# Attention of 32 heads in row blocks of 4 heads x 32 queries instead of 1 head x 128 queries, with the output projection per 128 tokens of all four heads

## The chip, the core and the metric

The kernel runs on one core of one Trainium2 chip, in one launch. The metric is the time of an execution on the device in microseconds (us). The time of the kernel before is 1990.96 us, the median of three runs (1986.2 to 1993.41). The engines are called PE (TensorE, matrix products), DVE (VectorE), ACT (ScalarE), POOL (GpSimd) and SP (SyncE, which here only issues DMAs). Lines such as L83 are lines of the kernel before.

## The reference

The model has two layers over x of 2 batches x 1024 tokens x 512. Layer 0 adds to the normed input's residual a single-head attention (d = 128) and a mixture of four streams, whose weights come from 50 Sinkhorn iterations. Layer 1 adds a grouped causal attention and a feed-forward block with eight low-rank experts, of which each token takes two. Nearly all of the time goes into the attention of layer 1: 32 query heads of 128, in 8 groups of four heads that share keys and values.

```python
def _L1_attn_ref(hidden_states, Wq, Wk_down, Wv_down, Wk_up, Wv_up, Wo):   # 2 x 1024 x 512
    H, HK, D = (32, 8, 128)
    q = (hidden_states @ Wq.T).reshape(b, s, H, D).transpose(0, 2, 1, 3)
    ...                       # k, v: down to 256 latent values, up to 8 heads of 128
    k = jnp.repeat(k, n_rep, axis=1)          # n_rep = 4
    v = jnp.repeat(v, n_rep, axis=1)
    scores = jnp.einsum('bhqd,bhkd->bhqk', q, k) * scale
    scores = jnp.where(causal, scores, jnp.asarray(-1000000000.0, scores.dtype))
    attn = jax.nn.softmax(scores, axis=-1)
    out = jnp.einsum('bhqk,bhkd->bhqd', attn, v)
    out = out.transpose(0, 2, 1, 3).reshape(b, s, H * D)
    return out @ Wo.T
xn = _layernorm(x, axis=-1)
x = x + _L0_attn_ref(xn, ...) + _L0_ffn_ref(xn, ...)
xn = _layernorm(x, axis=-1)
x = x + _L1_attn_ref(xn, ...) + _L1_ffn_ref(xn, ...)
```

## The kernel before

**Products.** Every product is made of three float16 passes over operands that are split into a high and a low part: high x high, high x low, low x high (`mm3`, L78 to L85). A result is taken out of PSUM by an eviction (`evac`, L97 to L99): ACT writes the high part, DVE the low part. Weights arrive as float32, by DMAs that POOL issues, and POOL splits them with three instructions (`split_pool`, L87 to L91: scale, high, low).

**A row step of attention** (`row_step`, L297 to L309) works on 128 partitions, which are 128 queries of one head. Block i of a head has 128(i+1) keys, so eight steps have widths 128, 256, ..., 1024.

1. `rows_scores` (L238): PE writes the scores into one or two PSUM tiles of up to 512 columns; there are four such tiles (tag `s`).
2. `rows_exp` (L251): DVE negates the scores and takes the running minimum, with the causal mask at the last piece (L260) and without it at an earlier one (L264). ACT takes the exponential and its sum (L268).
3. `rows_hi` (L272): DVE takes the reciprocal of the sum (L273), ACT scales it (L274) and writes the high part of the normed row, `Phl` (L281).
4. `rows_lo` (L284): DVE writes the low part (L290). A transposing DMA on SP (L292) brings the blocks of 128 x 128 of both parts to `PT`, with keys on the partitions.

A step issues its own scores and exponential together with the normalising (3 and 4) of the step before: first 1, then 3 for the older one, then 2, then 4 for the older one.

**Attention times V** (`attn_out`, L311) has V as weights and 512 queries of a head's half as moving columns: 12 products for the first half (keys up to 512) and 24 for the second, where the causal limit cuts the width to 512, 384, 256 or 128. `PTa` and `PTb` hold the transposed rows of the two halves, one buffer each. `head_av` (L631) evicts the result to `AO`.

**Layer 1** (`layer1_attn`, L637 to L711) goes through 64 heads (two batches), eight steps a head. Everything else is hung to a step ("slot") of a head by `at`, and `put` in the program does the same for work of other stages: the weight and the projection of the next head's Q (`load_q`, `q_half`), attention times V after slots 6 and 14 of a head, the next group's keys and values (`kv_next`) in the third head of a group, and, after the fourth head, eight blocks of the output projection (`wo_block`, L622: 12 products of 512 columns over the four heads' `AO`, then an addition to `acc` on DVE, L627, and in the last group the output's DMA on ACT's queue, L629). A batch thus has 8 groups of 32 row steps; G0 to G7 are batch 0, G8 to G15 batch 1.

**The program** (L822 to L903) runs layer 0's front for both batches, the Sinkhorn iterations of batch 0 on DVE, the stream mix, and the latents; those of batch 1's Sinkhorn (on POOL), its stream mix, its normalisation and the expert blocks are hung into the slots of layer 1. Between the batches (G7 to G8) the normed activations of batch 1 (`xT`) are made, and their latents.

**Order.** The tile framework orders the instructions of each engine when the kernel is built, by a timeline of its own (L947), from the order in which the code issues them, their dependencies and the free buffers. On the chip each engine works through its list in that order.

Of the kernel before, what the change touches and what calls it, by code (L numbers as in the profile page):

```python
# [9 lines left out]
F16 = mybir.dt.float16  # L10
# [6 lines left out]
P = 128  # L17
S = 1024
NB = 2
# [9 lines left out]
FB, HB, PB, LB, XB = 4, 4, 3, 3, 4  # L29
# [9 lines left out]
QA, QB, QNA, QNB, AA, AB = 0, 4, 4, 4, 6, 14  # L39
WA, WB, KV, KVN, LQ, LW = 12, 16, 4, 13, 5, 5  # L40
# [6 lines left out]
def tile_model(ctx: ExitStack, tc: tile.TileContext, out: bass.AP, a: dict):  # L47
    """Products run as three float16 passes over operands split into a high and
    a low part (hi*hi + hi*lo + lo*hi), each scaled by a power of two."""
# [25 lines left out]
    # passes over (lhs part, rhs part)  # L75
    PASSES = ((0, 0), (0, 1), (1, 0))

    def mm3(dst, pairs):  # L78
        """dst += sum over pairs of lhsT.T @ rhs, in three passes each."""
# [7 lines left out]
    def split_pool(stage, hl_hi, hl_lo, scale):  # L87
        """stage is scaled in place; its parts go to hl_hi and hl_lo."""
        G.tensor_scalar(stage, stage, scale, 1.0, ALU.mult, ALU.mult)  # L89
        G.tensor_scalar(hl_hi, stage, 1.0, 1.0, ALU.mult, ALU.mult)  # L90
        G.tensor_tensor(hl_lo, stage, hl_hi, ALU.subtract)  # L91
# [11 lines left out]
    # ---------------------------------------------------------- constants  # L103
    mask = C("mask", [P, 512])
    G.memset(mask, 0.0)
    G.affine_select(mask[:, 384:512], mask[:, 384:512], [[-1, P]],
# [3 lines left out]
    pm = C("pm", [P, 8])           # 8 - e  # L110
# [10 lines left out]
    # first layer's operands  # L121
# [13 lines left out]
    wo0 = T("wo", [P, 2, H], F16, bufs=4)  # L135
# [16 lines left out]
    bo = T("wo", [1, 2, H], F16, bufs=4)  # L152
# [8 lines left out]
    def split_w0b():  # L161
# [5 lines left out]
        # g = 1/(1+exp(-gate)), 1-g = exp(-gate) g; both over 4, for 4*xn  # L167
# [5 lines left out]
    # ---------------------------------------------------------- helpers  # L173
# [3 lines left out]
    def after(*insts):  # L177
        """issues what follows behind each of insts on its engine."""
# [5 lines left out]
    def rsqrt(y, ve, tag):  # L184
        """y = ve ** -0.5; ve > 0."""
# [8 lines left out]
    def layernorm(b, tag):  # L194
        """rows of acc[b, :]: mean and variance, 1/std, -4 mean/std, 4/std."""
# [17 lines left out]
    def normed_T(b, mv, rs, t, dst, pool, tags=(("f2k", FB), ("h2k", HB))):  # L213
        """dst[p, 2c+part, tok] of 4*(x-mean)/std."""
# [15 lines left out]
    def proj_T(w, xT, half):  # L230
        """psum[m, tok] of one half of the tokens; w(c, part) is [128 f, m]."""
# [6 lines left out]
    def rows_scores(Q, K, i, causal):  # L238
        """scores of the query rows of block i: (offset, width, psum) pieces."""
        W = P * (i + 1) if causal else S  # L240
        pieces = [(0, W)] if W <= 512 else [(0, W // 2), (W // 2, W // 2)]
        got = []
        for o, w in pieces:
            count[0] += 1
            pt = ps.tile([P, 512], F32, tag="s", name=f"s_{count[0]}", bufs=BS)
            mm3(pt[:, :w], [(lambda l: Q[:, l, i * P:(i + 1) * P],
                             lambda r: K[:, r, o:o + w])])
# [3 lines left out]
    def rows_exp(pieces, causal, scale):  # L251
        """exp(score - max) and its sums."""
# [19 lines left out]
    def rows_hi(Pm, r, W, pool):  # L272
        V.reciprocal(r[:, 1:2], r[:, 0:1])  # L273
        A.activation(r[:, 1:2], r[:, 1:2], AF.Copy, scale=PSCALE)  # L274
        hl = T("Phl", [P, NT, 2, P], F16, bufs=LB)
        p3 = Pm[:, :W].rearrange("p (j k) -> p j k", k=P)
        if pool:
            A.activation(Pm[:, :W], Pm[:, :W], AF.Copy, scale=r[:, 1:2])
            A.activation(hl[:, :W // P, 0, :], p3, AF.Copy)
        else:  # L280
            A.activation(hl[:, :W // P, 0, :], p3, AF.Copy, scale=r[:, 1:2])  # L281
        return hl

    def rows_lo(Pm, r, W, pool, hl, dst):  # L284
        n = W // P
        p3 = Pm[:, :W].rearrange("p (j k) -> p j k", k=P)
        if pool:
            G.tensor_tensor(hl[:, :n, 1, :], p3, hl[:, :n, 0, :], ALU.subtract)
        else:
            V.scalar_tensor_tensor(hl[:, :n, 1, :], p3, r[:, 1:2], hl[:, :n, 0, :],  # L290
                                   ALU.mult, ALU.subtract)
        nc.sync.dma_start_transpose(dst[:, 0:2 * n, :],  # L292
                                    hl[:, :n].rearrange("p j l k -> p (j l k)"))
# [3 lines left out]
    def row_step(Q, K, i, causal, scale, dst, pool):  # L297
        """one block of rows, a step ahead of the normalising of the last one."""
        if Q is not None:
            pieces = rows_scores(Q, K, i, causal)  # L300
        if pending:
            *what, d = pending.pop()
# [648 lines left out]
```

## Time and profile before

| what | value |
|---|---|
| median of three runs | 1990.96 us (1986.2, 1990.96, 1993.41) |
| the profiled execution's own time | 1993.41 us |
| its span | 1993.4 us |
| G0's first score product | 297.7 us after the span's start |
| G1 to G7, first score products | 391.7, 490.8, 587.2, 688.9, 799.7, 890.1, 1001.9 us |
| G8 (batch 1) to G15 | 1168.0, 1261.4, 1358.6, 1454.7, 1550.7, 1648.1, 1745.0, 1841.0 us |
| last product of PE | ends at 1989.6 us |

The profile is one execution. Its busy times by engine say how full an engine is; the slices say when. A group of instructions has the line, the engine, the operation, what it writes and reads with partitions x elements, a count, its busy time and the mean of one, and then the idle time of that engine just before those instructions, with what ended most of it. Some groups join several widths ("+3 forms"). The chain of work that ended last begins with these shares:

```profile
PE 33%; DVE 28%; issue 12%; ACT 12%; DMA 10%; POOL 5%; SPq 0%; DVEq 0%; ACTq 0%; POOLq 0%
```

Two rows of DMA issues matter for the change. Their columns are the transfer, the queue, the operation, the count and the median time from issue to landing in us:

```profile
PTb<-Phl SPq DMA_TRANSPOSE x272, 3.6
...
PTa<-Phl SPq DMA_TRANSPOSE x256, 2.6
```

### The profile page before, as it was taken

What the parts mean: (1) busy time and instruction counts of PE and PEld (TensorE: products, weight loads), DVE (VectorE), ACT (ScalarE), POOL (GpSimd) and SP (SyncE); (2) the same over time, 40 slices, a digit from 0 to 9 for tenths busy, and PEclk for the clock granted to TensorE, in tenths of its full rate; (3) what the DMA queues carried; (4) which work ended last, traced back from release to release, by engine and by line L of the source; (5) the groups of instructions that cost most, each with busy time, mean ns of one, the idle gap of its engine ahead of it and who ended that gap; (6) DMA issues with size and microseconds to landing.
All of it is one profiled execution on the core that took longest, in us unless ns stands there. A gap on an engine that the chain in (4) does not pass through costs nothing.

```text
span 1993.4 us, 32134 instructions
## 1 busy us (share of the span) xinstructions
PE 1779.4 (89%) x10210; PEld 920.4 (46%) x10210; DVE 1570.5 (79%) x4340; ACT 1219.5 (61%) x2902; POOL 871.7 (44%) x1178
## 2 busy tenths in 40 slices
PE   4365389899999998999999799999999999999998
PEld 2223134445455444554545355454545454545454
DVE  8999969988888787778875757777777777777755
ACT  3445456567576888674663646766666666666543
POOL 6644585866666656234710634141514142326010
PEclk9777699999999998999999999999999999999999
DMA  7131354656555565566643836555556575656524
GB/s 197 32 73 28 79 113 88 144 116 133 126 121 122 116 132 111 106 133 132 145 104 65 182 95 149 116 123 120 121 119 138 105 135 110 138 117 151 102 55 125
DMA packets 707293, 230.08 MB, mean 115 GB/s; under 512 B 689953, under 2 KB 690081, under 8 KB 707122
## 3 DMA queue, kind: packets, MB, share of 16 engines
q1 hardware_dynamic: 691666, 180.75, 44.1%
q0 software_dynamic: 13152, 43.07, 8.3%
q10 hardware_dynamic: 2304, 4.20, 0.6%
q8 instruction: 81, 1.33, 0.3%
q14 instruction: 90, 0.74, 0.1%
HBM read 52.81 MB, written 4.19 MB: 29 GB/s over the span
## 4 chain that ended last, share of the span: by engine, by line
PE 33%; DVE 28%; issue 12%; ACT 12%; DMA 10%; POOL 5%; SPq 0%; DVEq 0%; ACTq 0%; POOLq 0%
PE pp L83 19%; PE av L319 8%; PE s L83 6%; DVE Phl L290 6%; DMA PTb<-Phl 5%; ACT Phl L281 5%; DVE P L260 4%; ACT P L268 4%; DVE P L264 4%; DVE sk L501 2%; DVE sk L507 2%; DMA PTa<-Phl 2%; DVE acc L544 1%; DVE sk L512 1%; DVE sk L493 1%
## 5 line engine op out<-in xcount | busy, mean ns | idle before, releaser
L268 ACT ACTIVATE P<-P,nm 128x1024 f32<-128x1024 f32 (+7 forms) x528 | 412.3, 781 | 374.8 <-DVE nm L260 338.7
L290 DVE SCALAR_TENSOR_TENSOR Phl<-P,r,Phl 128x1024 f16<-128x1024 f32 (+7 forms) x520 | 492.3, 959 | 161.9 <-ACT Phl L281 160.2
L83 PE MATMUL s<-K,Q 128*128 128x384 f16 (+5 forms) x2400 | 486.9, 333 | 71.3 <-DVE P L264 49.1
L281 ACT ACTIVATE Phl<-P,r 128x1024 f16<-128x1024 f32 (+7 forms) x520 | 399.3, 777 | 65.9 <-DMA PTb<-Phl 44.4
L83 PE MATMUL pp<-xT,wq 128*128 128x512 f16 x1632 | 381.4, 380 | 4.7 <-POOL wq L91 2.2
L83 PE MATMUL pp<-wo,AO 128*128 128x512 f16 x1536 | 361.2, 380 | 1.4 <-DVE acc L627 0.7
L83 PEld LDWEIGHTS <-Q 128*128 128x128 f16 x2400 | 227.4, 99 | 276.1 <-issue 98.8
L319 PE MATMUL av<-PTb,V 128*128 128x512 f16 (+3 forms) x1632 | 325.0, 348 | 13.7 <-DMA PTb<-Phl 11.2
L319 PEld LDWEIGHTS <-V 128*128 128x128 f16 x2400 | 229.0, 99 | 234.4 <-issue 26.0
L83 PEld LDWEIGHTS <-wq 128*128 128x128 f16 x1632 | 158.0, 98 | 175.5 <-POOL wq L91 3.0
L83 PEld LDWEIGHTS <-AO 128*128 128x128 f16 x1536 | 149.7, 98 | 167.2 <-issue 3.9
L89 POOL TENSOR_SCALAR f2k<-f2k 128x512 f32<-128x512 f32 x164 | 115.8, 708 | 159.6 <-DMA f2k<-in_WoT 89.0
L90 POOL TENSOR_SCALAR wo<-f2k 128x512 f16<-128x512 f32 x64 | 43.7, 686 | 301.5 <-PE pp L83 300.5
L260 DVE CUSTOM_DVE_ANT_0 P<-s,mask,nm 128x320 f32<-128x320 f32 (+3 forms) x256 | 163.6, 640 | 12.6 <-PE s L83 6.3
L264 DVE TENSOR_SCALAR_CACHE_REDUCE P<-s 128x512 f32<-128x512 f32 (+3 forms) x272 | 158.5, 584 | 7.7 <-PE s L83 6.5
L273 DVE RECIPROCAL r<-r 128x1 f32<-128x1 f32 x528 | 81.4, 155 | 100.1 <-ACT P L268 98.0
L274 ACT ACTIVATE r<-r 128x1 f32<-128x1 f32 x528 | 98.9, 193 | 94.4 <-DVE r L273 93.8
L90 POOL TENSOR_SCALAR wq<-f2k 128x512 f16<-128x512 f32 x68 | 47.5, 699 | 224.3 <-PE pp L83 223.7
L319 PE MATMUL av<-PTa,V 128*128 128x512 f16 (+3 forms) x768 | 117.8, 304 | 11.0 <-DVE AO L99 10.9
L260 DVE CUSTOM_DVE_ANT_0 P<-s,mask 128x128 f32<-128x128 f32 (+3 forms) x256 | 121.2, 479 | 6.3 <-PE s L83 5.6
L83 PE MATMUL pp<-cmp,xT 128*128 128x128 f16 (+2 forms) x768 | 93.3, 282 | 34.6 <-DMA xT<-h2k 21.3
L99 DVE SCALAR_TENSOR_TENSOR Q<-pp,Q 128x512 f16<-128x512 f32 x128 | 87.1, 682 | 19.2 <-ACT Q L98 18.8
(226 smaller groups left out, 2215.7 us busy)
## 6 DMA issues: line engine op xcount, KB each, us to landing
f2k<-in_Wq POOLq DMA_DIRECT2D x64, 256.0 KB, 3.5
f2k<-in_WoT POOLq DMA_DIRECT2D x64, 256.0 KB, 3.3
PTb<-Phl SPq DMA_TRANSPOSE x272, 3.6
acc<-in_x SPq DMA_DIRECT2D x16, 256.0 KB, 4.5
xr<-in_x SPq DMA_DIRECT2D x16, 256.0 KB, 3.2
f2k<-in_Wup POOLq DMA_DIRECT2D x16, 256.0 KB, 3.5
PTa<-Phl SPq DMA_TRANSPOSE x256, 2.6
out<-acc ACTq DMA_DIRECT2D x16, 256.0 KB, 2.3
```

The source lines that it names most:

```text
L83: nc.tensor.matmul(dst, lhs(l), rhs(r), start=(i == 0 and j == 0), stop=(i == n - 1 and j == 2))
L89: G.tensor_scalar(stage, stage, scale, 1.0, ALU.mult, ALU.mult)
L90: G.tensor_scalar(hl_hi, stage, 1.0, 1.0, ALU.mult, ALU.mult)
L99: return V.scalar_tensor_tensor(hl_lo, src, scale, hl_hi, ALU.mult, ALU.subtract)
L260: last_row[0] = V.tensor_tensor_reduce(Pm[:, o:o + w], pt[:, :w], mask[:, 512 - w:], -scale, first, ALU.add, ALU.min, nm[:, k:k + 1])
L264: last_row[0] = V.tensor_scalar(Pm[:, o:o + w], pt[:, :w], -scale, first, ALU.mult, ALU.min, accum_out=nm[:, k:k + 1])
L268: A.activation(Pm[:, :W], Pm[:, :W], AF.Exp, bias=last, scale=-1.0, accum_out=r[:, 0:1])
L273: V.reciprocal(r[:, 1:2], r[:, 0:1])
L274: A.activation(r[:, 1:2], r[:, 1:2], AF.Copy, scale=PSCALE)
L281: A.activation(hl[:, :W // P, 0, :], p3, AF.Copy, scale=r[:, 1:2])
L290: V.scalar_tensor_tensor(hl[:, :n, 1, :], p3, r[:, 1:2], hl[:, :n, 0, :], ALU.mult, ALU.subtract)
L319: nc.tensor.matmul(p[:, q0:, :], Vh(j, l), PT[:, q0:, 2 * j + r, :], start=(j == 0 and k == 0), stop=(j == nj - 1 and k == 2))
```

## The change

**Row blocks.** A row step of layer 1 now holds 32 queries of all four heads of a group on its 128 partitions, query first, head second. A group has 32 steps as before, with widths 32, 64, ..., 1024 instead of four times 128, ..., 1024. To have such a block side by side, Q is kept per half of the tokens as [128, part, query, head]; a head's projection is evicted with four elements between neighbouring queries. The mask changes with it (bfloat16, limits by query).

**Padding and transposes.** Rows whose width is no multiple of 128 are filled up with zeros by a POOL memset (`rows_pad`; 384 in the program, none where the width is a multiple of 128). `Phl` now has all high parts ahead of all low parts. The transposing DMA of a step writes its blocks into one of two places of a `PT` tile that two steps share ([128, blocks, 2, 128]); there are three such tiles instead of one `PTa` and one `PTb`.

**Attention times V** is done for each pair of steps: 256 columns, and V for all key blocks up to the pair's chunk of 128 tokens. Two pairs make a chunk, which is evicted to `ao` [128, part, query, head].

**The output projection** is done for each chunk of 128 tokens as soon as its four heads are there, nine steps after the chunk's first row step (`WOD`), with `ao` read at a distance of four elements as weights, instead of eight blocks after the group's last head.

**Order.** The hung work is placed anew over the 32 steps of a group: Q projections of the second half in steps 1 to 10, those of the next group's first half from step 18, its keys and values in pieces from step 1, its weights of Q in steps 6 to 18 and those of the output projection in steps 34 to 40. The buffers change: weights of Q 4 (were 2), of the output projection 5 (were 4), `h2k` 3 (were 4).

**Around it.** The first four weights of Q and the first weights of keys and values are loaded ahead of batch 0's stream mix. The branch of layer 0 sums its four streams at once and keeps the sum; for batch 1 its addition to `acc` moves from ahead of layer 1 into slots of G0. The second batch's normed activations and latents, and the expert blocks, move to other slots. Layer 0's attention uses the new `PT` and `attn_out`, too. Comments fall away.

```diff
-    def rows_scores(Q, K, i, causal):
-        W = P * (i + 1) if causal else S
+    def rows_scores(q, K, W):
...
-            mm3(pt[:, :w], [(lambda l: Q[:, l, i * P:(i + 1) * P],
-                             lambda r: K[:, r, o:o + w])])
+            mm3(pt[:, :w], [(q, lambda r: K[:, r, o:o + w])])
...
+    def rows_pad(W):
+        n = -(-W // P)
+        hl = T("Phl", [P, 2 * S], F16, bufs=LB)[:, :2 * n * P].rearrange("p (l k) -> p l k", l=2)
+        if W < n * P:
+            G.memset(hl[:, :, W:], 0.0)
+        return hl
...
-            V.scalar_tensor_tensor(hl[:, :n, 1, :], p3, r[:, 1:2], hl[:, :n, 0, :],
+            V.scalar_tensor_tensor(hl[:, 1, :W], Pm[:, :W], r[:, 1:2], hl[:, 0, :W],
                                    ALU.mult, ALU.subtract)
-        nc.sync.dma_start_transpose(dst[:, 0:2 * n, :],
-                                    hl[:, :n].rearrange("p j l k -> p (j l k)"))
+        nc.sync.dma_start_transpose(dst, hl.rearrange("p l k -> p (l k)"))
...
         for j in range(nj):
-            q0 = max(0, j - 4 * half) if causal else 0
             for k, (l, r) in enumerate(PASSES):
-                nc.tensor.matmul(p[:, q0:, :], Vh(j, l), PT[:, q0:, 2 * j + r, :],
+                nc.tensor.matmul(p, Vh(j, l), PT[:, r * nj + j].rearrange("p a b -> p (a b)"),
...
-    def qproj(b, w, Q, half):
+    def qproj(b, w, Q, hh, half):
         p = proj_T(lambda c, l: w[:, l, c, :], xT1[b], half)
-        evac(p, Q[:, 0, sl], Q[:, 1, sl], 0.125)
+        evac(p, Q[:, 0, :, hh], Q[:, 1, :, hh], 0.125)
...
-        mm3(p, [(lambda l, q=q: AOs[q][:, l, q0:q0 + P],
-                 lambda r, q=q: wos[q][:, r, :]) for q in range(4)])
+        mm3(p, [(lambda l, h=h: ao[:, l, :, h],
+                 lambda r, h=h: wos[h][:, r, :]) for h in range(4)])
...
+    def group_av(Vh, PT, c, k, p):
+        attn_out(p[:, 256 * k:256 * k + 256], lambda j, l: Vh[:, l, j, :], PT, c + 1)
+        if k == 0:
+            return None
+        ao = T("ao", [P, 2, P, 4], F16, bufs=2)
+        hi, lo = [ao[:, l].rearrange("p q h -> p (q h)") for l in range(2)]
+        evac(p, hi, lo, 1.0 / PSCALE)
...
+            for u in range(4):
+                at(g, QH + 3 * u, lambda g=g, u=u: q_unit(g, 4 + u))
+            for c in range(NT):
+                for k in range(2):
+                    at(g, 4 * c + 2 * k + AVD, lambda g=g, c=c, k=k: av(g, c, k))
+                at(g, 4 * c + WOD, lambda g=g, c=c: wo(g, c))
...
+                    c, r = divmod(s, NR)
+                    if r % 2 == 0:
+                        PTs[g, s // 2] = T("PT", [P, 2 * (c + 1), 2, P], F16, bufs=3)
+                    Qt, q0 = Qs[g, s // (NS // 2)], s % (NS // 2) * QR
+                    row_step(lambda l: Qt[:, l, q0:q0 + QR].rearrange("p q h -> p (q h)"),
+                             kvs[g]["K"], QR * (s + 1), True, SC1, PTs[g, s // 2][:, :, r % 2], False)
...
-    with tc.issue_after(last_pool[0].ins):
-        for t in range(NT):
-            branch0_add(1, t, y4s[t], f0[1][4])
...
+    for t in range(NT):
+        put(1, 2 * t, lambda t=t: branch0_add(1, t, y4s[t], f0[1][4]))
```

with `QR = 32`, `AVD, WOD = 5, 9` and `KVN, QN, QNN, QH = 16, 18, 24, 1`.

## The prediction

> **What bounds the kernel now.** I read the page's engine shares and its 40 slices first: they say which engine is full, and when.
>
> ```profile
> PE 1779.4 (89%) x10210; PEld 920.4 (46%) x10210; DVE 1570.5 (79%) x4340; ACT 1219.5 (61%) x2902; POOL 871.7 (44%) x1178
> ...
> PE   4365389899999998999999799999999999999998
> ...
> PEclk9777699999999998999999999999999999999999
> ```
>
> PE is half empty in the first six slices (layer 0) and full in nearly all others, at a full granted clock. The second view cuts the span at the first score product of each group of four heads (G0 starts at 298 us, G7 at 1002, G8 at 1168, G9 to G14 lie between 1261 and 1841, G15 is last).
>
> ```profile
> 0.00:298.00 298.00, 160.16 (x901) 83.77 (x902) 268.09 (x981) 141.09 (x348) 169.80 (x193) 0.78 0.37 87
> 298.00:392.00 94.00, 85.86 (x567) 43.64 (x566) 89.60 (x231) 57.48 (x142) 66.22 (x107) 1.00 0.52 115
> ...
> 1261.00:1841.00 580.00, 567.12 (x3244) 294.79 (x3242) 444.72 (x1129) 383.90 (x888) 189.47 (x234) 1.00 0.59 125
> 1841.00:1993.00 152.00, 142.04 (x785) 72.21 (x783) 91.89 (x237) 69.55 (x155) 11.13 (x14) 0.97 0.44 97
> ```
>
> Columns: stretch, its length, busy us of PE, PEld, DVE, ACT, POOL, granted clock, DMA share, GB/s. A plain group takes 580/6 = 96.7 us, and PE is busy for 98% of it. Layer 0 is DVE's (268 of 298 us). So 85% of the time is bounded by what PE has to stream.
>
> Busy time hides the price of one product, since products overlap. The timeline of PE gives it:
>
> ```profile
> 288.57 2.84 PE L83 MATMUL pp<-h2k,cmp 128*128 128x128 f16 x48
> ...
> 338.66 1.33 PE L83 MATMUL pp<-gw,xT 128*128 128x32 f16 x47
> ...
> 1971.73 6.63 PE L83 MATMUL pp<-wo,AO 128*128 128x512 f16 x30 [0.35 <-DVE acc L627]
> 1978.20 4.38 PE L319 MATMUL av<-PTb,V 128*128 128x512 f16 x24
> ```
>
> Thirty 512-wide products last 6.63 us, of which 0.38 is the last one alone: (6.63 - 0.38)/29 = 216 ns each. The 128-wide cost (2.84 - 0.22)/47 = 56 ns, the 32-wide (1.33 - 0.18)/46 = 25 ns. That is (columns + 5.5)/2.4 ns, with a floor of 25. The last line (15 of 512 columns, three each of 384, 256, 128) gives 4.38 by it too. Each product here brings its own weight load, so a load is inside these prices.
>
> The rows of one block of queries, by shape:
>
> ```profile
> L290 DVE SCALAR_TENSOR_TENSOR Phl<-P,r,Phl 128x1024 f16<-128x1024 f32 x72 | 100.7, 1399 | 45.1 <-ACT Phl L281 44.7
> ...
> L264 DVE TENSOR_SCALAR_CACHE_REDUCE P<-s 128x512 f32<-128x512 f32 x80 | 53.8, 675 | 4.9 <-PE s L83 4.8
> L260 DVE CUSTOM_DVE_ANT_0 P<-s,mask,nm 128x512 f32<-128x512 f32 x64 | 47.2, 737 | 0.2
> ...
> L290 DVE SCALAR_TENSOR_TENSOR Phl<-P,r,Phl 128x128 f16<-128x128 f32 x64 | 28.8, 450 | 6.7 <-ACT Phl L281 6.7
> ```
>
> L290 thus costs about 1.06 ns a column and 0.33 us besides; the minimum passes 1.03 a column and 0.15 to 0.21, with an 81 ns read. ACT's two passes go from 390 ns (128 columns) to 1145 (1024).
>
> **The change part by part.** Every group keeps 32 row steps, 144 score products and 8 evictions of each kind.
>
> 1. *Scores.* The columns of a group fall from 4 x 4608 = 18,432 to 32 x 528 = 16,896. PE: 1536 x 3 / 2400 = 1.9 us a group. DVE passes twice over each column: 1536 x (1.03 + 1.06) = 3.2 us. ACT twice: 2.6 us.
> 2. *Attention times V.* The columns stay 18,432; 144 products become 216 of 256 columns. 72 x 2.3 ns = 0.2 us more. The sum of both is -1.7 us a group, **-27 us** over 16, all on the bounding engine; adding all products of both programs by the formula gives 1705.7 and 1678.3. [...]
> 3. *Balance inside a group.* Work sums in us per eight row steps, by the rows above (evictions 0.68 DVE, 0.58 ACT), every function put at its slot. Before: PE 27.2, 27.2, 22.2, 16.9 against DVE 22.0, 22.0, 22.0, 19.2; the larger of both adds up to 95.9, and 96.7 is measured, so 0.8 is waits. After: PE 21.7, 17.8, 24.3, 28.1 = 91.8, DVE 13.6, 17.2, 23.8, 27.4: PE is the larger everywhere, but in the last 16 steps by 2% only. The fullest DVE of a layer-1 stretch above is 89.6 of 94 us, 95%. At 95% those 16 steps take 51.2/0.95 = 53.9 instead of 52.4: +1.5. A plain group: 91.8 + 0.8 + 1.5 = 94.1, that is 0.9 below what PE's saving alone leaves. For the 12 groups without stage work of their own: **-11 us**. Bounds: nothing added (-2.4 a group, -29) and DVE at 90% (+2.1 a group, +25).
> 4. *Last group.* No next group: its last 16 steps lack four Q projections, PE 42.0, DVE 48.5. **+6.5 us** (0 to 10). The tail behind the last scores stays about equal: 9.4 us of chain (minimum passes, exponential, two scalings, L290, a 3.5 us transposing DMA) against 7.5 of products there.
> 5. *Memsets.* 384 more on POOL. Nearest rows: 98 ns for one column, 206 for 128 f16 columns; mean about 0.21, 79 us in all, hidden: POOL goes from 44 to 48%. What is queued behind a late one is the step's DMA on SP, every later DMA there, then the product with V. Cover: from a pair's last score product to its first product with V PE has 17.0 us of work in the median (17.6 before), the chain takes 9.4. In the built order three weight writes of wo that wait for the last output block of the group before stand ahead of step 8's memset: 5 us of POOL, inside that cover.
> 6. *DMAs.* The blocks stay (288 a group), the issues too (528), all on SP in the same order; a step's blocks now land 512 B apart instead of side by side. No row shows that.
>
> ```profile
> q1 hardware_dynamic: 691666, 180.75, 44.1%
> ```
>
> The packets are 261 B already, one row of a block each, so I take 0. Ends: the cheapest and dearest queue of the page, per MB, differ by 1.7 (q10 0.6% for 4.20 MB, q1 44.1% for 180.75), so 0.6 to 1.7 times today's price.
> 7. *Strided stores and weights.* Q is stored with 4 elements between neighbours, ao read so as weights. No row. Weights: the row is 98 ns a load beside a 216 ns product, so free until 2.2 times dearer; above that 1536 loads pay. Stores: between 0 and a second pass, 0.68 us on DVE for four evictions in the last 16 steps, 2.8 a group, +45. I take 0 for both: nothing in the rows tells patterns apart (an eviction that reads every second column costs 376 ns for 256 columns, on the line of the others).
> 8. *Layer 0 and the batch border.* DVE, which bounds layer 0, gets 2 evictions more ahead of the first row. Five weight loads (13 us of POOL) move ahead of the stream mix, where POOL has gaps, 18 us of adds leave to G0, two Q projections (5.2 us) come earlier. The border's work gets 16 steps instead of 8 to hide in. I take 0, between -10 and +10.
>
> Sum: 1993.4 - 27 - 11 + 6.5 = 1962. The span equals the slowest of the three times shown (1993.41), with nothing around it; the median is 2.4 lower. So for a median run **1960 us**.
>
> **The rivals.**
> - *DVE takes over* (0.15). For it: 98% of PE in half of each group, and the score tiles (4) let PE run only two wide steps ahead. Against: 76% over a whole plain group today. With DVE at 90%: -27 + 25 + 10 gives 2001 at worst, about **1985**.
> - *The transposing DMAs bind; slower* (0.10). Place: the last eight steps of a group, whose 120 blocks now come together. A block costs 44.1% x 1993 x 0.0328/180.75 = 0.159 us, so 19.1 us, and 3.4 of other DMAs (0.59 x 96.7 - 45.8 = 11.2 a group, by share), against 28.1 of PE. It decides once a block is dearer by 1.29. At 1.5: +3.9 a group, +62, **2022 us**. Against: 691,666 packets of one row. [...]
> - *Strided stores are dear* (0.09): +45, **2005 us**.
> - That the change does not do what it says is excluded by the built program: its shapes are 32, 64, ... 1024 columns.
>
> **How the numbers follow.** Forecast 0.66, with its own range 1930 to 1981. About 0.5% (10 us) is what this measurement can tell from no change. Faster by more: 0.66 and 0.06 of the first rival, 0.72. Same: the rest of the first rival and 0.02 of the third, 0.11. Slower: 0.10 + 0.07 = 0.17. The low end 1925 is the balance bound (-29) with -10 of layer 0 and no loss at the end; the high end 2010 takes in the first and third rivals and leaves the DMA case out.
>
> **What would show it.** A plain group of about 94 us (93 to 95); PE over 96% busy there; columns 1678 us by the formula; L290 at 0.33 us + 1.06 ns a column; Q evictions at 682 and 581 ns; loads of ao near 98 ns; issue to landing of the DMAs near 3.2 us in late steps. Wrong if PE waits in the last 16 steps of each group for minimum passes (first rival) or DMAs (second), if Q evictions are dearer (third), or if G0 starts after 310 us.

## The result, and the profile after

The changed kernel takes 2081.51 us (median of four, 2075.98 to 2089.01) against 1988.58 us for the kernel before on the same chip: ratio 1.0458, 95% interval 1.0424 to 1.0492. It is **slower by 4.6%**; forecast was 1960 us, faster by 1.5%. The profiled execution spans 2074.2 us, 80.8 more than before. From its page, engine shares and slices:

```profile
PE 1780.3 (86%) x11458; PEld 1080.6 (52%) x11458; DVE 1613.3 (78%) x4340; ACT 1257.4 (61%) x2902; POOL 912.5 (44%) x1562
...
PE   2564369889989898989699899999999999999997
...
PEclk8777589999999999999899899999999999999999
```

PE is no busier than before in us, in a longer span. The cut by stretches (G0 now starts at 326 us, G9 at 1361, G15 at 1943; columns as before):

```profile
0.00:326.00 326.00, 168.63 (x1021) 96.48 (x1022) 277.93 (x982) 145.71 (x350) 171.13 (x209) 0.76 0.35 85
326.00:433.00 107.00, 93.90 (x646) 53.90 (x644) 97.98 (x246) 61.62 (x143) 72.02 (x127) 0.95 0.47 92
...
1361.00:1943.00 582.00, 559.81 (x3674) 349.77 (x3671) 460.00 (x1128) 393.26 (x888) 209.52 (x378) 1.00 0.57 124
1943.00:2074.00 131.00, 120.46 (x788) 74.44 (x785) 81.12 (x222) 65.84 (x148) 9.96 (x30) 0.98 0.49 103
```

Six plain groups take 582 us instead of 580, PE being busy for 96% instead of 98%. The groups of instructions hold the largest single reason, with the memsets and weights that the prediction spoke of:

```profile
L278 POOL MEMSET Phl<- 128x192 f16 (+2 forms) x384 | 78.0, 205 | 740.6 <-DMA PT<-Phl 567.1
...
L85 PEld LDWEIGHTS <-ao 128*128 128x128 f16 x1536 | 169.7, 115 | 187.4 <-ACT ao L100 40.2
...
L101 DVE SCALAR_TENSOR_TENSOR Q<-pp,Q 128x512 f16<-128x512 f32 x128 | 166.9, 1304 | 56.6 <-ACT Q L100 50.4
L100 ACT ACTIVATE Q<-pp 128x512 f16<-128x512 f32 x128 | 167.8, 1311 | 47.5 <-PE pp L85 47.2
```

The same rows in the kernel before (what is `ao` now was called `AO`):

```profile
L83 PEld LDWEIGHTS <-AO 128*128 128x128 f16 x1536 | 149.7, 98 | 167.2 <-issue 3.9
...
L99 DVE SCALAR_TENSOR_TENSOR Q<-pp,Q 128x512 f16<-128x512 f32 x128 | 87.1, 682 | 19.2 <-ACT Q L98 18.8
...
L98 ACT ACTIVATE Q<-pp 128x512 f16<-128x512 f32 x128 | 74.0, 581 | 43.0 <-PE pp L83 41.1 <-PE s L83 1.3
```

An eviction of Q, 682 and 581 ns before, takes 1304 and 1311 ns: storing every fourth element takes 1.9 times as long on DVE and 2.3 times on ACT. `ao`, stored side by side, still takes 687.

Where the 80.8 us are, by first score products (us). "e4" is the fourth experiment, with side-by-side runs:

| stretch | before | after | e4 |
|---|---|---|---|
| up to G0 | 297.7 | 326.3 | 329.6 |
| G0 to G3 (iterations of batch 1 beside) | 391.2 | 427.2 | 417.3 |
| G4 to G7 (mix, experts, border) | 479.1 | 510.9 | 493.9 |
| G8 to G14 | 673.0 | 678.3 | 651.9 |
| G15 to the end | 152.4 | 131.5 | 130.6 |

PE's time from G0 on can be split for each product: its price by the formula of the prediction, and what the next one starts later than that, put down to that next product (us):

| | before | after | e4 |
|---|---|---|---|
| price of the products | 1579.5 | 1545.6 | 1545.6 |
| late: scores | 50.9 | 78.7 | 53.1 |
| late: output projection | 4.4 | 47.7 | 35.0 |
| late: Q projection | 7.8 | 23.7 | 14.3 |
| late: attention times V | 33.3 | 27.4 | 25.1 |
| late: others | 15.8 | 20.8 | 16.7 |

The price fell by 33.9 us (5.2 of it are two Q projections that now lie ahead of G0), so the saving came. PE's waits rose by 86.1, and layer 0 by 28.6: -33.9 + 86.1 + 28.6 = 80.8.

Not all of the 86.1 is standing still. From G0 on, PE's granted clock falls to one half in 20 stretches, of 3.4 to 10.2 us (92 us in all; 9 stretches and 44 us before). In the 8 us ahead of each, PE had stood for 24 to 52% of the time (26 to 41% before), and in them products of 512 columns come 427 ns apart instead of 216. Of the lateness in the table, 39.9 us lie in such stretches, 20.3 before. So about 20 of the 86.1 us lie in stretches at half the clock; that PE's waits bring these about is the author's reading, and no run shows it apart.

### The profile page after: what moved, and what is told of

It reads as the page before. It is cut to its first block, busy times and chain, and to the rows that moved or that the text cites. A ratio compares the mean times of both kernels' runs of the same rounds, so it can differ in the third digit from the quotient of the medians.

```text
span 2074.2 us, 35602 instructions
## 1 busy us (share of the span) xinstructions
PE 1780.3 (86%) x11458; PEld 1080.6 (52%) x11458; DVE 1613.3 (78%) x4340; ACT 1257.4 (61%) x2902; POOL 912.5 (44%) x1562
## 3 DMA queue, kind: packets, MB, share of 16 engines
q1 hardware_dynamic: 691666, 180.75, 42.6%
## 5 line engine op out<-in xcount | busy, mean ns | idle before, releaser
L269 ACT ACTIVATE P<-P,nm 128x1024 f32<-128x1024 f32 (+31 forms) x528 | 391.3, 742 | 369.6 <-DVE nm L261 302.2
L294 DVE SCALAR_TENSOR_TENSOR Phl<-P,r,Phl 128x1024 f16<-128x1024 f32 (+31 forms) x520 | 478.0, 927 | 141.4 <-ACT Phl L288 136.0
L85 PE MATMUL s<-K,Q 128*128 128x512 f16 (+22 forms) x2400 | 448.4, 325 | 134.8 <-DVE P L265 102.1
L321 PE MATMUL av<-PT,V 128*128 128x256 f16 x3648 | 450.9, 277 | 30.0 <-DMA PT<-Phl 23.2
L288 ACT ACTIVATE Phl<-P,r 128x1024 f16<-128x1024 f32 (+31 forms) x520 | 379.2, 735 | 72.0 <-DMA PT<-Phl 54.3
L85 PE MATMUL pp<-wo,ao 128*128 128x512 f16 x1536 | 382.3, 386 | 31.8 <-ACT ao L100 24.4
L85 PEld LDWEIGHTS <-ao 128*128 128x128 f16 x1536 | 169.7, 115 | 187.4 <-ACT ao L100 40.2
L101 DVE SCALAR_TENSOR_TENSOR Q<-pp,Q 128x512 f16<-128x512 f32 x128 | 166.9, 1304 | 56.6 <-ACT Q L100 50.4
L100 ACT ACTIVATE Q<-pp 128x512 f16<-128x512 f32 x128 | 167.8, 1311 | 47.5 <-PE pp L85 47.2
L261 DVE CUSTOM_DVE_ANT_0 P<-s,mask,nm 128x272 f32<-128x272 f32 (+15 forms) x256 | 157.2, 615 | 13.3 <-PE s L85 3.0
L283 ACT ACTIVATE r<-r 128x1 f32<-128x1 f32 x528 | 98.8, 195 | 103.9 <-DVE r L282 103.1
L265 DVE TENSOR_SCALAR_CACHE_REDUCE P<-s 128x512 f32<-128x512 f32 (+15 forms) x272 | 152.8, 563 | 8.0 <-PE s L85 6.9
```

The costliest lines, as they stand in the source:

```text
L85: nc.tensor.matmul(dst, lhs(l), rhs(r), start=(i == 0 and j == 0), stop=(i == n - 1 and j == 2))
L100: A.activation(hl_hi, src, AF.Copy, scale=scale)
L101: return V.scalar_tensor_tensor(hl_lo, src, scale, hl_hi, ALU.mult, ALU.subtract)
L261: last_row[0] = V.tensor_tensor_reduce(Pm[:, o:o + w], pt[:, :w], mask[:, 512 - w:], -scale, first, ALU.add, ALU.min, nm[:, k:k + 1])
L265: last_row[0] = V.tensor_scalar(Pm[:, o:o + w], pt[:, :w], -scale, first, ALU.mult, ALU.min, accum_out=nm[:, k:k + 1])
L269: A.activation(Pm[:, :W], Pm[:, :W], AF.Exp, bias=last, scale=-1.0, accum_out=r[:, 0:1])
```

## The experiments

Theory after the result: the strided stores are dear, and DVE, taken to be nearly full in a group's later steps, has no room for them. First rival: POOL's order, in layer 0 and G0.

**e1: Q stored side by side.**

```diff
-        evac(p, Q[:, 0, :, hh], Q[:, 1, :, hh], 0.125)
+        hi, lo = [Q[:, l].rearrange("p q h -> p (q h)")[:, 512 * hh:512 * hh + 512] for l in range(2)]
+        evac(p, hi, lo, 0.125)
```

> The changed kernel, but the evictions of Q store their 512 columns side by side instead of four elements apart. It leaves out the order of Q (queries and heads end in wrong places), nothing else. In the changed kernel such an eviction takes 1304 ns on DVE and 1311 ns on ACT, against 682 and 581 before. Theory (strided stores are the cause of most of the loss): both fall back to about 680 and 580 ns, that is 5.0 us of DVE and 5.8 us of ACT less in each group; a plain group (G9 to G14) falls from 97 us to 94, and the groups G0 to G5, which take 47 us more in all than in the kernel before, lose most of that too: about 2000 us. Rival (the loss outside the plain groups comes from the order of the work on POOL, not from the stores): plain groups fall to 94, G0 to G5 keep at least 30 of the 47 us, G0 still starts at 326 us minus 3: about 2045 us.

2033.98 us, ratio 1.0232 (1.0193 to 1.0270); evictions 683 and 586 ns. Plain groups take 93.6 us (97.0 in the changed kernel), but G0 to G5 still 624.2 (639.3 there, 592.4 before) and G0 starts at 325.7. The stores of Q alone cost 2.3%, some 45 us, about half of the loss; the rest lies elsewhere, as the rival says.

**e2: the first weight loads back behind batch 0's mix and latents.**

```diff
-    for hh in range(4):
-        load_q(0, hh)
-    kv0 = kv(0, 0)
-    kv0[1][0]()
     new_xT(0)
...
     latents(0, wl)
+    for hh in range(4):
+        load_q(0, hh)
+    kv0 = kv(0, 0)
+    kv0[1][0]()
```

> The changed kernel, with the first weight loads (four of Q, one of keys and values) again behind the stream mix and the latents of batch 0. Theory (POOL's order in layer 0: in the changed kernel the first adds of the stream mix on POOL start 24 us later, behind these weight splits): the first score product of G0 comes 15 to 28 us earlier than 326.3 us, the rest stays: 2055 us. Rival (G0 comes late because of four Q evictions at 1.3 us instead of two at 0.6, and of the products of layer 0's attention ahead of the latents): G0 starts at most 8 us earlier, 2070 us or more.

2069.11 us, 1.0401 (1.0375 to 1.0428); G0 at 320.4, 5.9 us earlier, so the rival's size. The trace shows more. POOL's timeline at the stream mix, in the changed kernel:

```profile
209.53 0.83 POOL L540 TENSOR_SCALAR xr<-xr,rsa 128x512 f32<-128x512 f32 x1 [14.38 <-DMA xr<-in_x]
210.34 1.14 POOL L93 TENSOR_TENSOR wq<-f2k,wq 128x512 f16<-128x512 f32 x1
211.48 0.76 POOL L540 TENSOR_SCALAR xr<-xr,rsa 128x512 f32<-128x512 f32 x1
212.22 1.25 POOL L547 TENSOR_TENSOR acc<-acc,f2k 128x512 f32<-128x512 f32 x1
```

The mix's adds (L547) stand behind weight splits and a wait of 14.4 us. They start at 212 us; in the kernel before (L540) and in e2 (L547) their first rows are these:

```profile
187.70 6.76 POOL L540 TENSOR_TENSOR acc<-acc,f2k 128x512 f32<-128x512 f32 x5 [8.37 <-ACT f2k L539]
```

```profile
189.18 6.94 POOL L547 TENSOR_TENSOR acc<-acc,f2k 128x512 f32<-128x512 f32 x5 [3.83 <-ACT f2k L546]
```

e2 gets that back, but its eighth normed tile then stands behind the moved splits and a missing buffer (`h2k` 3 instead of 4), and PE waits 17.9 us for it.

**e3: the branch's addition back ahead of layer 1** (the two edits of the change's last diff lines undone).

> The changed kernel, with the addition of batch 1's branch to its accumulator again ahead of layer 1 instead of in slots of G0. Theory (POOL's load in G0 is the cause of the 13 us that G0 takes more than before): G0 falls from 107 to under 100 us and G0's start moves by less than 5 us: 2065 us. Rival (G0 to G3 are slow because DVE has the strided stores beside the second batch's iterations): G0 stays at 105 to 109 us, and the time stays within 5 us of 2081 or rises as far as the adds hold up POOL in layer 0.

2080.50 us, 1.0463 (1.0431 to 1.0496): nothing. G0 falls to 98.8 us, as the theory said, and G2 and G3 by 8.5 in all; but G1 rises by 2.8, G4 and G5 by 7.6, G8 to G14 by 8.0. The time is the rival's, its G0 (105 to 109 us) is not: what G0 gains is lost later.

**e4: rows in the order head, query.** Q is stored in runs of 32, the mask is made for each head's 32 rows, and the product with V writes its columns by head, so that `ao` is read side by side, too.

```diff
-T("Q", [P, 2, S // 2, 4], F16, bufs=2)
+T("Q", [P, 2, S // 2 // QR, 4, QR], F16, bufs=2)
...
-        evac(p, Q[:, 0, :, hh], Q[:, 1, :, hh], 0.125)
+        evac(p.rearrange("p (b q) -> p b q", q=QR), Q[:, 0, :, hh], Q[:, 1, :, hh], 0.125)
...
-        attn_out(p[:, 256 * k:256 * k + 256], lambda j, l: Vh[:, l, j, :], PT, c + 1)
+        attn_out(p.rearrange("p (h b q) -> p b h q", h=4, b=NR)[:, 2 * k:2 * k + 2],
+                 lambda j, l: Vh[:, l, j, :], PT, c + 1, True)
```

> The changed kernel with the rows of a block in the order head, query instead of query, head: an eviction of Q then stores runs of 32 elements (64 bytes) instead of single elements four apart, the products with V write four runs per step into PSUM, and the weights of the output projection lie side by side. The output is the reference's. Theory (single strided elements are what makes the store dear): Q evictions at 680 and 580 ns, as with stores side by side; plain groups 94 us, and the time within 10 us of that of the run with side-by-side stores. Rival (any break in the row makes the store dear, or products that write in runs of 32 are dearer): Q evictions stay over 1000 ns, or a product with V of 256 columns takes over 115 ns instead of 109, and the time stays within 15 us of 2081.

2027.23 us, 1.0194 (1.0163 to 1.0226). Rows of the groups in e4:

```profile
L85 PEld LDWEIGHTS <-ao 128*128 128x128 f16 x1536 | 146.4, 98 | 194.1 <-ACT ao L100 31.5 <-issue 5.7 <-ACT P L270 2.9
...
L101 DVE SCALAR_TENSOR_TENSOR Q<-pp,Q 128x512 f16<-128x512 f32 x128 | 87.2, 681 | 30.0 <-ACT Q L100 29.6
...
L100 ACT ACTIVATE Q<-pp 128x512 f16<-128x512 f32 x128 | 75.0, 586 | 55.3 <-PE pp L85 54.9
```

Runs of 64 bytes cost what side by side costs (683 and 586 ns in e1), and a product with V of 256 columns is no dearer: the mean record is 277 ns, as in the changed kernel, and three in a row in G0 take 0.49 us in e5, which has e4's runs, and in the changed kernel. The strided layout is worth 1.0458 - 1.0194, **2.6% or some 52 us**. That holds the stores of Q (some 45 us by e1) and the reading of `ao`; the intervals of e1 and e4 overlap, so that the reading costs anything is not shown. Plain groups now take 92.6 us, below the 94.1 of the forecast; what e4 still loses lies ahead of G8. For the 14.8 us that it loses in G4 to G7 no run here gives the cause; e12, without the iterations, takes 494.5 us there, no less than e4.

**e5: e4 with e2's edit, and another buffer (`wo`) for the eighth tile.**

```diff
-        normed_T(b, *ln1[b], t, xT1[b][:, t], pool)
+        normed_T(b, *ln1[b], t, xT1[b][:, t], pool,
+                 (("f2k", FB), ("wo", WB) if b == 0 and t == 7 else ("h2k", HB)))
```

> The version with runs of 32 (2027 us, G0's first score product at 329.6 us), with the first weight loads again behind the stream mix and the latents, and with a buffer of the weights of the output projection for the eighth tile of batch 0's normed activations (they had four buffers in the kernel before, three in the changed one; with the loads moved alone, the eighth tile came 15 us late, behind weight splits on POOL). Theory (layer 0 loses its 30 us by what stands on POOL ahead of the stream mix's adds and of the last tile): G0 starts at 300 to 308 us, 2003 us. Rival (the loads are only a part; the products of layer 0's attention and four Q projections ahead of G0 keep it late): G0 at 315 us or later, 2013 us or more.

2012.08 us, 1.0084 (1.0051 to 1.0116), 1.1% or some 22 us less than e4. G0 starts at 314.8 us, nearly the rival's 315. Of the 17 us still lost, 5.2 are the two Q projections that must now be there, and the last latent products start 9.4 us later (278.0 against 268.6).

**e6: the iterations early in each group.**

```diff
-        put(0, SK0 + k * SKN // 51, chain_step)
+        put(0, 32 * (k // 13) + 1 + (k % 13), chain_step)
```

> The version with runs of 32, with the 51 steps of batch 1's iterations in steps 1 to 13 of each of G0 to G3 instead of evenly over nearly four groups. Theory (the changed kernel has DVE at 26 us of each 28 in the last 16 steps of a group, so that the iterations' DVE work there, some 10 us a group, has no cover; in the first 16 steps it has): G1 to G3 fall from 104.7, 104.7 and 103.1 us to 97 to 100 each, G0 by some 4: about 2008 us. Rival (G0 to G5 are slow because the output projection, now soon after the rows, waits for its evictions on ACT): G1 to G3 stay within 2 us, 2027 us.

2037.16 us, 1.0208 (1.0157 to 1.0258), G1 to G3 311.6 us in all (312.5 in e4). Inconclusive: in the trace the iterations lie almost where they did (DVE's part in G1 by quarters of eight steps: 5, 6, 9, 13 instructions, in e4 5, 6, 9, 15), since each step waits for the one before on POOL.

**e7: the output projection two steps later** (`WOD = 11`).

> The version with runs of 32, with the output projection of a chunk 11 steps after its first row step instead of 9. Theory (in G0 to G3 the products wait 17 us in all for ACT's evictions of the product with V, made only two steps earlier): that wait falls below 6 us and the time to about 2015 us. Rival (the wait only stands for DVE being late; another product waits instead): the wait ahead of the output projection falls and that ahead of the scores rises, and the time stays within 5 us of 2027.

2051.07 us, 1.0287 (1.0266 to 1.0307): slower. G1 to G3 fall by 13.7 us in all, but G0 rises by 7.8 and plain groups from 92.6 to 97.3. Ahead of the output projection PE's lateness in G0 to G3 falls from 17.0 to 10.6; in the plain groups that ahead of it and of attention times V rises. Neither forecast: the wait is real, and neither of the two places suits both kinds of group.

**e8: widths rounded up to 128** (`P * (c + 1)` instead of `QR * (s + 1)` as the width).

> The version with runs of 32, with the widths of the row steps rounded up to multiples of 128 (columns of a group from 16,896 back to 18,432; the memsets of padding are gone). The causal mask then stands at the end of the rounded width, so that it hides other keys; that is left wrong. Theory (the saved columns are worth what PE has to stream, 1.9 us a group): plain groups go from 92.2 to 94.1 us, the time to 2027 + 30 = 2057 us. Rival (DVE sets the pace in the last 16 steps, and each saved column is worth two passes of DVE there): plain groups go to 95.5 us and the time to 2075 us; and should the memsets on POOL hold up the rows, part of that comes back.

2068.62 us, 1.0377 (1.0355 to 1.0398). The price of the products rises by 30.2 us (1545.6 to 1575.8), the theory's 30; the plain groups rise by 5.7 us, to 98.3, more than even the rival said. So a column saved is worth more than PE's share of it; DVE's two passes over it are the likely reason, but stand here together with all else that the widths change. G0 to G3, where POOL now has no memsets, fall by 13.1 us although their products cost 7.6 more, and DVE's wait for POOL's part of the iterations falls there from 34.5 to 12.3 us. That points to the memsets beside the iterations; but the widths changed with them, so it is not shown.

**e9: the memset a step later** (`rows_pad` called beside `rows_hi`).

> The version with runs of 32, with the memset of a row step's padding (and its Phl buffer) issued one step later, together with the normalising that fills the buffer. In G0 to G3 POOL waits 57 us for the transposing DMA that has to leave the buffer before the memset, and DVE then waits 34 us for POOL's part of batch 1's iterations (12 us in the kernel before, 12 us with padded widths, which need no memset). Theory (memsets that wait block POOL, POOL holds the iterations, these hold DVE's queue with the rows behind): POOL's wait for the DMA falls below 20 us, DVE's for POOL below 20 us, G0 to G3 fall by 12 to 25 us in all, the ratio to the kernel before from 1.019 to 1.008 to 1.013. Rival (DVE waits for POOL because POOL has more to do there, additions of the branch and memsets themselves, not because it is blocked): POOL's wait falls, DVE's stays at 30 us, the ratio at 1.017 to 1.021; and the memset, now later, may hold up the transposing DMA of its own step: 1.02 or more.

2034.37 us, 1.0205 (1.0172 to 1.0239). It tells nothing of the memsets: POOL's order stayed, its wait for the DMA was 60 us. But two plain groups of this run differ. G12 and G13, the same work:

```profile
1610.50:1702.50 92.00, 92.00 (x615) 57.04 (x613) 69.43 (x188) 62.09 (x150) 32.76 (x60) 1.00 0.60 130
1702.50:1800.90 98.40, 94.58 (x614) 57.07 (x612) 76.93 (x188) 61.57 (x149) 32.53 (x60) 0.98 0.60 121
```

Third number after the length is DVE: the same 188 instructions take 7.5 us more. DVE's timeline, first in G13, then in G12:

```profile
1722.47 3.25 DVE L295 SCALAR_TENSOR_TENSOR Phl<-P,r,Phl 128x256 f16<-128x256 f32 x1
```

```profile
1630.23 0.47 DVE L295 SCALAR_TENSOR_TENSOR Phl<-P,r,Phl 128x256 f16<-128x256 f32 x1
```

During the 3.25 us POOL runs four weight-split instructions (the first began before) and a memset back to back; the row's low part ends with them. POOL in G13:

```profile
1722.02 1.15 POOL L93 TENSOR_TENSOR wo<-f2k,wo 128x512 f16<-128x512 f32 x1
1723.14 0.61 POOL L91 TENSOR_SCALAR f2k<-f2k 128x512 f32<-128x512 f32 x1
1723.72 1.15 POOL L93 TENSOR_TENSOR wo<-f2k,wo 128x512 f16<-128x512 f32 x1
1724.85 0.61 POOL L92 TENSOR_SCALAR wo<-f2k 128x512 f16<-128x512 f32 x1
1725.40 0.25 POOL L279 MEMSET Phl<- 128x192 f16 x1
```

In G12 POOL has the same splits in a row there, but the row's low part comes at the end of one, runs at once, and POOL's next takes longer:

```profile
1629.06 1.29 POOL L93 TENSOR_TENSOR wo<-f2k,wo 128x512 f16<-128x512 f32 x1
1630.32 0.87 POOL L91 TENSOR_SCALAR f2k<-f2k 128x512 f32<-128x512 f32 x1
```

So in G13 DVE's instruction stands beside POOL's (3.25 us against 0.47), and in G12 POOL's beside DVE's (0.87 us against 0.61); the two places differ in which began first. Over the plain groups of the versions with runs of 32 and the output projection at 9 steps there (e8 and e16 apart), DVE's low parts lose 2 to 11 us a group above 0.21 us + 1.05 ns a column (the short ones of this run: 0.47 us for 256 columns, 0.65 for 416); seven groups that lose 9 or more take 96.8 to 99.6 us, those that lose under 5 take 92.0 to 94.0 but for one of 95.9. The two go together; no run takes the splits away to show the cause. The kernel before loses 3.6 to 5.1 in its plain groups; how it would bear 9 is not shown.

**e10, e11: e5 with e9's edit; and with the output projection at 11 steps in G0 to G3.**

> Runs of 32, the layer-0 order of the run that gave 1.008, and the later memset. Theory: the gains add up, 1.0084 - 0.008 = 1.000 of the kernel before (0.995 to 1.004). Rival (the memset is not the cause, or DVE then waits for something else in G0 to G3): 1.006 to 1.010.

> The same, with the output projection 11 steps after a chunk's first row step in G0 to G3 and 9 elsewhere (with 11 everywhere, G1 to G3 fell by 13.7 us in all, but G0 rose by 8 and every plain group by 3 to 5). Theory (in G0 to G3 the projection waits for evictions that ACT makes late because DVE is late): 5 to 10 us less than the version without this edit, ratio 0.993 to 0.998. Rival (once the memset no longer blocks POOL, that wait is gone and the later slot only costs): the same or up to 5 us more.

2015.64 us, 1.0110 (1.0083 to 1.0137), and 2021.87 us, 1.0153 (1.0115 to 1.0191). Both come out nearest the rivals: e9's edit does nothing, and e11 gains 21 us in G1 to G3 over e5 in its profile, loses 8 in G0, and is not faster.

**e12, e13: e4 and the kernel before without most of batch 1's iterations.**

```diff
-        for it in range(1, 50):
+        for it in range(1, 50 if b == 0 else 3):
```

> The version with runs of 32, without the iterations of batch 1 after the third (its stream mix uses unfinished weights). Theory (the iterations' work on DVE and POOL has no cover in the last 16 steps of a group): G1 to G3 fall from 104.7, 104.7 and 103.1 us to 92 to 95, like the plain groups. Rival (POOL's memsets or the output projection's wait for its evictions make these groups slow, whatever the iterations): G1 to G3 stay at 100 us or more.

> The kernel before, without the iterations of batch 1 after the third. Theory (there the iterations lie under PE, which is fuller than DVE in each part of a group): G1 to G3, 99.1, 96.4 and 101.7 us, change by 3 us at most each, to 96 to 98. Rival (the iterations cost the kernel before as much as the changed one): they fall by 5 us or more, below the 96.7 us of a plain group.

1997.62 and 1988.31 us, a single run each. The third group (G2), in e4, in e12, in the kernel before and in e13:

```profile
539.10:643.80 104.70, 94.78 (x615) 57.17 (x613) 77.53 (x215) 61.89 (x147) 63.05 (x141) 0.98 0.57 114
```

```profile
527.20:619.20 92.00, 92.00 (x615) 57.01 (x612) 71.34 (x188) 62.27 (x150) 32.85 (x60) 1.00 0.60 127
```

```profile
491.00:587.00 96.00, 94.56 (x540) 48.70 (x537) 79.95 (x217) 62.69 (x149) 62.66 (x123) 1.00 0.56 124
```

```profile
490.50:586.60 96.10, 94.28 (x542) 49.28 (x541) 75.40 (x188) 63.98 (x149) 29.67 (x36) 1.00 0.58 124
```

Without the iterations G2 falls by 12.7 us in the new scheme, to a group in which PE never waits, and not at all in the old one, though 4.6 us of DVE and 33 of POOL leave it. G0 to G3 go from 417.3 to 384.0 us in e12 and from 391.2 to 392.6 in e13: **the iterations cost 33 us in e4's scheme and nothing before**. (The runs of e6, e9 and e10, which have the iterations, take 417 to 419 us for G0 to G3, too.) G1 alone keeps 101.0 us, so the theory's 92 to 95 holds for two of three.

**e14, e15: the memset behind ACT's high part (on e4); and with e5's edits, the output projection at 11 steps in G1 to G3.**

```diff
+            with tc.issue_after(hi.ins):
+                G.memset(hl[:, :, W:], 0.0)
```

> The version with runs of 32, with each padding memset placed behind ACT's high part of the same row, which has itself waited for the buffer (the edit with a step later had left POOL's order as it was). Theory (waiting memsets hold up POOL's share of the iterations, and these DVE): POOL's wait for the transposing DMA in G0 to G3 falls from 57 to under 20 us, DVE's wait for POOL from 34 to under 20, and G1 to G3 by 3 to 6 us each. Rival (POOL has slack, the wait only moves): POOL's wait for the DMA falls but G1 to G3 stay within 2 us; the rows' DMAs may come later and cost PE waits for them ahead of the products with V.

> Runs of 32, the layer-0 order of e5, the memset behind ACT's high part, and the output projection 11 steps after a chunk's first row step in G1 to G3 alone. Theory (the repairs add up): e5's 1.008 less 16 us of G1 to G3, ratio 0.998 to 1.002. Rival (they take from the same wait, or the memset costs): 1.004 to 1.010.

2022.13 us, 1.0143 (1.0120 to 1.0167), half a per cent below e4, the intervals just touching; and 2012.55 us, 1.0100 (1.0079 to 1.0121), no better than e5. In e14 POOL's wait for the DMA stays (56.6 us), DVE's for POOL falls from 34 to 24, and G1 to G3 by 4.8 in all. So the memsets' place matters by 10 us at most, hardly more than the noise; that it does so by POOL's wait, as supposed, is not shown.

**e16, e17: the iterations' reciprocals on POOL, as a power of -1.**

> Runs of 32, the layer-0 order of e5, the memset behind ACT's high part, and the reciprocals of batch 1's iterations on POOL (as a power of -1) instead of DVE; the output projection at 9 steps everywhere. Theory (DVE is full from step 8 on, and its share of the iterations, some 9 us a group with the waits for POOL, goes onto the time): G1 to G3 fall to 93 to 97 us, and the ratio to the kernel before from 1.008 to 0.990 to 0.997, faster than both kernels. Rival (POOL's reads and its blocked queue are the cause): G1 to G3 stay over 100 us or rise, the ratio at 1.006 or more.

> The kernel before, with the reciprocals of batch 1's iterations on POOL. Theory (its iterations lie under PE): the ratio stays within 0.996 to 1.003. Rival (DVE's share costs there, too): 0.985 to 0.995.

2391.27 us, 1.2034 (1.2002 to 1.2066), and 2375.92 us, 1.1964 (1.1925 to 1.2002). Such a power takes 5477 ns for 32 columns on POOL (98 of them 536.7 us), and G4 of e16, where batch 1's mix waits for them, takes 486 us. G1 to G3 of e16 take 291.0 us, but with fewer iterations in them; whether it is DVE's or POOL's share of the iterations that costs stays open.

No version of the whole program made here beats the kernel before; e5 comes nearest.

## Why the prediction was wrong, by its steps

1. *Scores* and 2. *attention times V*: right. -27 us was forecast; the price of PE's products fell by 33.9 - 5.2 = 28.7. A product of 256 columns takes 109 ns, as the formula has it: in the changed kernel 48 of them last 5.40 us, of which 0.28 is the last one alone. "At a full granted clock" was read from slices that hide short stretches at half of it: 44 us of them from G0 on before, 92 after.
3. *Balance*: right where it was used, and **used too narrowly**. With cheap stores a plain group takes 92.6 us (94.1 forecast), and PE is the larger in each quarter. But the step spoke only "for the 12 groups without stage work of their own". By its own sums PE leads DVE by 2 to 3% from step 8 on; the iterations that come on top in G0 to G3 got no term. They were hidden before and cost 33 us in e4's scheme (e12, e13). Why is open: cut at the first score products of the steps, DVE is busy for 22.4 us beside 29.0 of PE in the third quarter of e4's plain groups and 22.9 beside 28.1 in the last, and for 28.1 of 34.4 and 25.6 of 29.3 us in G0 to G3. So DVE is not full by its busy time, and its waits for POOL, and POOL's memsets (e8), may be as much a part of it. (The 0.33 us that the prediction reads for a low part, 0.31 by its two rows, is read from means, 450 ns for 128 columns and 1399 for 1024, that hold long ones, too; by the medians in the kernel before, 346 and 1285 ns, it is about 0.21.)
4. *Last group*: +6.5 forecast, -20.9 measured from G15 to the end. Missed: of a group's eight output blocks, which ran beside the next group's rows, six now run in their own group. Behind G15's first score product stand 120 products of them instead of 184, and the price of all products there falls from 136.4 to 117.7 us; G0 has 72 of them instead of 2 and is 13.2 us longer. What remains of the -20.9 is 2.2 us less waiting, so the +6.5 did not come.
5. *Memsets*: 205 ns and 78 us in all, as forecast. "Hidden" holds in the plain groups of e4 (92.6 us with the memsets); in G0 to G3 it is doubtful (e8), and e14's later place gained 10 us at most.
6. *DMAs*: right. The queue took 42.6% of 2074 us, 884 us, for the packets that took 44.1% of 1993, 879 us. Blocks 512 bytes apart show no loss there, and the median from issue to landing is 3.4 us (2.6 and 3.6 before).
7. *Strided stores and weights*: **the step that failed most**. It took "0 for both"; the upper end, "a second pass, 0.68 us on DVE", was the truth (+0.62 on DVE, +0.73 on ACT for each of 128). That rival had +45 us (0.68 x 4 x 16 is 44) and 9 chances in 100; the stores alone cost some 45 (e1), with the reading of `ao` some 52 (e4). The weights are the other half: 115 ns instead of 98, and whether a product of 216 ns hides that wholly is not shown apart. The row that the step leaned on, an eviction that reads every second column at no cost, is one of reading; these stores are another pattern and did not behave like it.
8. *Layer 0*: 0, between -10 and +10, forecast; +28.6 measured. "Where POOL has gaps" was read from POOL's busy share; the adds of the mix were next in POOL's queue and came 24 us later, and the normalisation and the latents need what they make. With the adds back in time G0 came only 5.9 us earlier (e2), since another tile now stood behind the splits; with that mended, too, 14.8 us earlier than in e4 (e5), about half of the loss.

Added up from the runs: 80.8 less 51 (e4), less 33 (e12), less the 32 that e4 loses ahead of G0, leaves -35 us against the -31.5 of the forecast sum (-27 - 11 + 6.5); by the whole time of e12, 27 below e4's, it is -29. So what it priced came in all, but not part by part, which is luck: G8 to G14 gain 21 us in e4, where about 18 follow from the forecast (2.6 a group), while G4 to G7 lose 14.8 instead of gaining, and the +6.5 did not come. Three things that had no cost in the sum took 116: the stores (a term put at 0), layer 0 (a term put at 0) and the iterations in G0 to G3 (no term). The rivals were held apart as alternatives, and the range ended at 2010. The third came at its price, and two of the prediction's own signs of being wrong showed, dearer Q evictions and G0 after 310 us; the first, DVE taking over, did not come in the plain groups.

## What to carry to other kernels

Work that an even load hides may lose its cover when a change makes one engine's total smaller but its load steeper. The 33 us of the iterations fit this, though the steps between are not shown. So ask for each stretch what is left beside the fuller engine, and then put all the other work of the stretch on top, not only in the stretches without any. A new access pattern with no row of its own should be priced at the dear end, or tried first by itself; runs of 32 elements gave `ao` side by side at no cost to the evictions of Q here (681 and 586 ns in e4, 682 and 581 in the kernel before). Work moved to a "free" place on an in-order engine is priced by who waits for the next thing in that queue (here the mix's adds, 24 us late).

## What the hardware showed that was not expected

- Stores of f16 with 8 bytes between neighbours, from PSUM: 1304 ns on DVE and 1311 on ACT for 512 columns; in runs of 64 bytes 681 and 586. Side by side they take 683 and 586 (e1).
- A low part of 256 columns on DVE stood through four weight-split instructions of POOL in a row (3.25 us against 0.47, e9), not only the one that ran when it came.
- Products of 256 columns that write PSUM in runs of 32 have a mean record of 277 ns (e4), like ones that write side by side in the changed kernel (277).
